# One memory for the rows of both graph-attention layers, and the first layer's softmax taken in groups

## The chip, the cores and the metric

The kernel runs on one core of a Trainium2 chip. The metric is the device time of one execution in microseconds (us). A core has five engines that run their own lists of instructions and meet at semaphores: TensorE (PE) multiplies matrices into PSUM, VectorE (DVE) and ScalarE (ACT) work elementwise on SBUF and PSUM, GpSimd (POOL) does small work and here mainly issues gathers, and SyncE (SP) issues plain DMA transfers. Everything is in 32-bit floats.

## The reference

The graph has 10,000 nodes with 768 features and 170,000 directed edges, sorted by destination and with self loops among them (the layer adds one more loop for each node). Two graph-attention layers follow each other, each with a layer norm and a residual product, and one last norm closes:

```python
def gat_conv(x, src, dst, W, a_src, a_dst, bias, heads):
    xl = (x @ W).reshape(n, heads, -1)
    e = leaky_relu((xl * a_src).sum(-1)[src] + (xl * a_dst).sum(-1)[dst], 0.2)
    e = exp(e - segment_max(e, dst)[dst])          # softmax over a node's edges
    alpha = e / (segment_sum(e, dst)[dst] + 1e-16)
    return segment_sum(xl[src] * alpha, dst) + bias

h1 = relu(layer_norm(gat_conv(x, W1, 4 heads x 256))) + (x @ Wr1 + br1)    # 1024 wide
h2 = layer_norm(gat_conv(h1, W2, 1 head x 768)) + (h1 @ Wr2 + br2)         # 768 wide
out = plain_norm(x + h2)
```

## The kernel before

The 10,000 nodes are put in order of their number of edges and cut into 79 tiles of 128 nodes. A tile has one node on each partition and as many **slots** as its busiest node has edges: slot k of a tile is a 128-row gather, row p being the features of the k-th neighbour of node p. There are 1377 slots in all, from 8 to 41 per tile.

**Three stages.** First x·W1 is computed for all nodes and stored as table 1 (a row has 1024 features, 4 + 4 attention terms and one more number, 1033 floats; 529 KB for 128 rows), while the order of the nodes is worked out beside it. Then layer 1 runs over the 79 tiles, gathers from table 1, and writes for each tile h1 and x (to `h1_d`, `x_d`) and a row of table 2 (770 floats; 394 KB for 128 rows). Then layer 2 runs over the tiles with gathers from table 2. The change touches layer 1 and the beginning of layer 2.

**Layer 1 for a tile of n slots.** In order of turn, n goes 8, 10, 11, ... up to 19 (turns 25 to 28), 20, 21 (32, 33), 22, 22, 23, 24, 26, 41 (turn 39), 27, 25, 24, 23, 22, 22, 21 (46) and down again to 9 (78). `Ring` holds the gathered rows in 29 slots that are reused round robin (`RING1`); `ring.fetch` on POOL (L425) issues the gather that refills a slot once the row in it has been weighed. The softmax weights of a tile come from `logits`: DVE adds the two terms of all n rows (L479), applies leaky relu (L189), takes the maximum (L483), subtracts it (L486), and ACT takes the exponential (L487); POOL copies the indices out and clears the row ends (L490, L491). `normalised` then divides by the sum (L504, L498 to L501). Since L479 reads all n rows, a tile's logits wait until its last row is in the ring.

The first four rows (`on_pe`) are summed on PE: ACT makes diagonal matrices of the weights (L730) and PE multiplies them with the rows into PSUM `acc` (L736). The others are summed by DVE in `weigh`: every fourth by four fused multiply-adds of 128x256 (L521), the other three of four by one 128x1024 addition (L517) after ACT has multiplied the row in place by its weights (L510). At the tile's end come the norm (L579, L581, L593, L595), relu and the residual (L807). PE also transposes h and x (L708), multiplies x by Wr1 (L172) and h by W2 (L829). The list of each engine is fixed in program order by the loop over k in `ordered_layer1`: three rows before the end of a tile (`LEAD`) stand the logits of the next tile, so that its first rows are ready when it begins.

**Tile 39** has 41 slots and the ring 29. It takes another way, `attend_parts`: the slots are cut into three groups, each with its own softmax whose sum is scaled to the new maximum (`fade`); nothing of the next tile is put into it, and the tiles 39 and 40 (27 slots, and 27 + `LEAD` is more than 29) do not get their logits ahead.

**From layer 1 to layer 2.** Layer 2's pool of buffers takes the memory of layer 1's, so its first instructions wait for the end of all of layer 1, the last of which is a store of table 2 (L768). Then SP loads h1 and x of the first two tiles of layer 2 (L911, L912), the tile's own row of table 2 (L454), and the broadcast vectors (L144); Wr2 is loaded earlier, into Wr1's place. DVE copies br1 out to a 128x1024 operand (L905), PE multiplies it by Wr2 (L172, 16 products), computes the residual of tile 0 (`residual`, L988 and L991: x + h1·Wr2), then, from the first rows, tile 0's sums (L946) and the residual of tile 1. Layer 2 has a ring of 41 slots (`RING2`), takes its tiles from few slots to many, and already has softmax groups, two for a tile of 26 slots or more (`cuts_of`, `PARTED2`). At the end of tile 0, DVE adds br1·Wr2 to a vector (L1066) from the PSUM buffer `q`.

Of the kernel before, what the change touches and what calls it, by code (L numbers as in the profile page):

```python
# [35 lines left out]
P = 128  # L36
BANK = 512
# [16 lines left out]
PARTED2 = 26  # L54

# [25 lines left out]
def gnn_kernel(ctx, tc, x, x_cols, src, dst, src_col, dst_col, W1, a_src1, a_dst1, b1, g1, be1, Wr1, br1,  # L81
# [359 lines left out]
    class Ring:  # L441
# [4 lines left out]
        def __init__(self, pool, table, row, size, own, at=None):  # L446
            self.table, self.size, self.own, self.issued = table, size, own, 0
            self.at = at or list(range(TOTAL))
            self.rows = pool.tile([P, size, row], F32, name="ring")
# [11 lines left out]

        def slot(self, q):
            return self.rows[:, q % self.size, :]

        def parts(self, lo, hi):

            while lo < hi:
                r = lo % self.size
                m = min(hi - lo, self.size - r)
                yield lo, lo + m, self.rows[:, r:r + m, :]  # L470
                lo += m
# [40 lines left out]
    def weigh(acc, row, e, dh, first=None, shared=False):  # L512


        if shared:
            c = e.shape[1] * dh
            nc.vector.tensor_add(acc[:, :c], acc[:, :c], row[:, :c])  # L517
            return
# [4 lines left out]

    def attend_parts(small, ring, acc, h_, ad, heads, dh, t, summed, between):


        c = heads * dh
        groups = -(-SLOTS[t] * 2 // ring.size)
        cuts = [FIRST[t] + SLOTS[t] * g // groups for g in range(groups + 1)]
        top = total = sums = None  # L530
        nc.vector.memset(acc[:, :c], 0.0)
        for lo, hi in zip(cuts, cuts[1:]):
            e, new = logits(small, ring, lo, hi, ad, heads, c, top)
            if lo == FIRST[t]:
                doubled(e, t)
            part = small.tile([P, heads], F32, name="part")
            nc.vector.reduce_sum(part, e.rearrange("p k h -> p h k"), axis=AX.X)
            if top is not None:
                nc.vector.tensor_add(acc[:, :c], acc[:, :c], sums[:, :c])
                fade = small.tile([P, heads], F32, name="fade")  # L540
                nc.vector.tensor_sub(fade, top, new)
                nc.scalar.activation(fade, fade, AF.Exp)
                for h in range(heads):
                    s = slice(h * dh, (h + 1) * dh)
                    nc.vector.tensor_scalar(acc[:, s], acc[:, s], fade[:, h:h + 1], None, op0=OP.mult)
                nc.vector.tensor_mul(fade, total, fade)
                nc.vector.tensor_add(part, part, fade)
            top, total = new, part
            m = min(ON_PE1, hi - lo - 1)
            pe = lo if hi == cuts[-1] else hi - m  # L550
            steps = summed(pe, e[:, pe - lo:], m)
            sums = next(steps)
            if pe == lo:
                for _ in steps:
                    pass
            alone = [q for q in range(lo, hi) if not pe <= q < pe + m]
            for k, q in enumerate(alone):
                shared = k >= len(alone) // 3
                if shared:
                    multiply(ring.slot(q), e[:, q - lo], dh)  # L560
                if k == len(alone) // 3 + 1:
                    for _ in steps:
                        pass
                weigh(acc, ring.slot(q), e[:, q - lo], dh, shared=shared)
                ring.fetch(q + 1 + ring.size)
            ring.fetch(hi + ring.size)
            between.pop(0)()
        nc.vector.tensor_add(acc[:, :c], acc[:, :c], sums[:, :c])
        divided(small, h_, acc, total, None, heads, dh)
# [111 lines left out]
    SLOTS1, FIRST1 = SLOTS, FIRST  # L681

# [3 lines left out]
    def ordered_layer1():  # L686
        nc.scalar.add_instruction(mybir.InstLoadActFuncSet(name=nc.get_next_instruction_name(), act_func_set_id=6, engine=nc.scalar.engine))
        with tc.tile_pool(name="b1", bufs=1) as pool, tc.tile_pool(name="small1", bufs=2) as small, \
# [3 lines left out]
            ring = Ring(pool, table1, R1, RING1, {})  # L692
# [25 lines left out]
            ring.fetch(RING1)  # L718
# [22 lines left out]
            def weights_of(t):  # L741

                n, m = SLOTS[t], on_pe(t)
                e, _ = logits(small, ring, FIRST[t], FIRST[t] + n, ring.slot(FIRST[t])[:, C1:C1 + H1], H1, C1)
                yield e
                normalised(small, e, H1, t)
                acc = ps_acc.tile([P, 2 * BANK], F32, name="acc")
                diagonals = pool.tile([P, ON_PE1 * H1, P], F32, name="diagonals")
                for lo, hi in ((0, min(m, 2)), (min(m, 2), m)):
                    summed(acc, diagonals, e, FIRST[t], lo, hi, m)  # L750
                    yield acc

# [18 lines left out]
            xT, moves = from_x(0)  # L771
            for move in moves:
                move()
            r = product(xT, wr1, C1, ps_r)
            for t in range(NT + 1):
# [3 lines left out]
                whole = live and n <= ring.size  # L779
                if whole and not ready:  # L780
                    ahead = weights_of(t)
                    ready += itertools.islice(ahead, 2)

                def multiplied(upto):
                    nonlocal done
                    while whole and done < min(upto, n):
                        if shared(t, done):
                            multiply(ring.slot(FIRST[t] + done), e[:, done], DH1)
                        done += 1

                if whole:
                    e, acc = ready
# [3 lines left out]
                for _ in ahead:  # L796
                    pass
# [544 lines left out]
```

## Time and profile before

| what | us |
|---|---|
| median of three runs | 5579.29 |
| the three runs | 5576.32, 5579.29, 5603.79 |
| the profiled execution: time | 5572.26 |
| the profiled execution: span in the trace | 5570.4 |
| first stage | 0 to 880 |
| layer 1 | 880 to 3412 |
| layer 2 | 3412 to 5570 |

| stage | PE busy | DVE busy | ACT busy | POOL busy | DMA share |
|---|---|---|---|---|---|
| first stage (880 us) | 844.63 | 481.76 | 353.62 | 422.02 | 0.38 |
| layer 1 (2532 us) | 2244.79 | 2196.78 | 1863.74 | 1544.97 | 0.91 |
| layer 2 (2158.4 us) | 1797.91 | 1591.10 | 597.77 | 1334.62 | 0.86 |

The profiled execution is 7.0 us below the median and 4.1 us below the fastest of the three runs. In the tables of the profile, "idle before" is the time in which an engine had nothing to run just before the group of instructions, and what stands behind the arrow is what ended it. Over all of layer 1, DVE waits 66.0 us in 12 waits for gathered rows at the logits (L479), and 46.5 us in 44 waits for PE's sum at the first row that it adds to it (L521).

### The profile page before, as it was taken

How to read it: one execution, taken by the hardware profiler on the slowest of the kernel's cores; microseconds unless marked ns; L12 is line 12 of the kernel's file. 1: busy time of each engine (PE TensorE's matmuls, PEld its weight loads, DVE VectorE, ACT ScalarE, POOL GpSimd, SP SyncE). 2: the span in 40 equal slices, each digit the busy share in tenths (PEclk: the TensorE clock that was granted, in tenths of full speed). 3: DMA queues.
4: the chain of work that ended last, by engine and by line, in shares of the span. 5: the costliest groups of instructions: out<-in, count | busy, mean ns of one | idle time of the engine just before them, and what ended most of it. 6: DMA issues, size and time to landing. Idle time of an engine off the chain costs nothing. (4 is left out here: it accounts for less than half of the span.)

```text
span 5570.4 us, 59760 instructions
## 1 busy us (share of the span) xinstructions
PE 4887.3 (88%) x15188; PEld 2896.9 (52%) x15191; DVE 4269.6 (77%) x7513; ACT 2815.1 (51%) x8193; POOL 3301.6 (59%) x3407
## 2 busy tenths in 40 slices
PE   9999996999999876689999999899988888887775
PEld 3444443555565544455555555565655555554544
DVE  5883344999999887789999995888876776766676
ACT  3443343777878776678877773333322222222222
POOL 2446455556666666566666653666665666666664
PEclk9999998999999987899999999999998888888887
DMA  4323536999999987899999986999888888888885
GB/s 156 123 94 89 91 97 234 323 345 354 364 366 371 350 325 255 314 342 369 370 367 361 339 310 230 334 336 329 323 322 287 307 298 301 295 291 294 293 293 183
DMA packets 474308, 1591.39 MB, mean 286 GB/s; under 512 B 118327, under 2 KB 122487, under 8 KB 473958
## 3 DMA queue, kind: packets, MB, share of 16 engines
q0 software_dynamic: 322384, 1286.62, 64.5%
q1 hardware_dynamic: 149520, 297.43, 15.8%
q10 hardware_dynamic: 2054, 3.42, 0.2%
q8 instruction: 128, 2.10, 0.1%
q14 instruction: 222, 1.82, 0.1%
HBM read 1431.80 MB, written 177.29 MB: 289 GB/s over the span
## 5 line engine op out<-in xcount | busy, mean ns | idle before, releaser
L425 POOL DMA_INDIRECT ring<-table,slots x2675 | 2664.3, 996 | 1631.5 <-issue 662.2
L521 DVE SCALAR_TENSOR_TENSOR acc<-ring,e,acc 128x512 f32<-128x512 f32 (+1 forms) x2530 | 1579.0, 624 | 149.4 <-PE acc L736 46.5
L510 ACT ACTIVATE ring<-ring,e 128x256 f32<-128x256 f32 x3284 | 1338.4, 508 | 2.3 <-issue 2.2
L517 DVE TENSOR_TENSOR acc<-acc,ring 128x1024 f32<-128x1024 f32 x801 | 986.5, 1232 | 70.5 <-DVE acc L517 1.4
L991 PE MATMUL big<-wr,w 128*128 128x512 f32 (+1 forms) x2464 | 872.0, 500 | 111.3 <-issue 109.8
L946 PE MATMUL big<-ring,diagonals 128*128 128x256 f32 x2754 | 758.5, 433 | 206.8 <-issue 168.0
L172 PE MATMUL big<-w,xT 128*128 128x512 f32 x1896 | 827.2, 598 | 23.3 <-DMA w<-in_W_dram 9.4
L172 PE MATMUL big<-wr,xT 128*128 128x512 f32 x1896 | 831.7, 595 | 0.2 <-issue 0.2
L829 PE MATMUL half<-w,hT 128*128 128x512 f32 (+1 forms) x2528 | 830.4, 486 | 0.0
L946 PEld LDWEIGHTS big<-ring,diagonals 128*128 128x128 f32 x2754 | 593.8, 219 | 371.5 <-issue 235.1
L991 PEld LDWEIGHTS big<-wr,w 128*128 128x128 f32 x2464 | 481.3, 196 | 471.4 <-issue 439.5
L945 ACT ACTIVATE diagonals<-ident,e 128x128 f32<-128x128 f32 x1377 | 423.5, 388 | 598.4 <-remote 180.3
L829 PEld LDWEIGHTS half<-w,hT 128*128 128x128 f32 x2528 | 477.8, 189 | 372.3 <-issue 334.4
L736 PE MATMUL acc<-ring,diagonals 128*128 128x256 f32 x1912 | 474.8, 406 | 201.9 <-ACT diagonals L730 198.0
L172 PEld LDWEIGHTS big<-w,xT 128*128 128x128 f32 x1896 | 362.7, 192 | 483.7 <-issue 464.9
L172 PEld LDWEIGHTS big<-wr,xT 128*128 128x128 f32 x1896 | 356.0, 191 | 419.4 <-issue 419.4
L736 PEld LDWEIGHTS acc<-ring,diagonals 128*128 128x128 f32 x1912 | 384.6, 204 | 285.0 <-ACT diagonals L730 219.0
L583 ACT ACTIVATE sd<-mv,eps 128x1 f32<-128x1 f32 x237 | 69.3, 293 | 696.9 <-DVE mv L581 444.4
L667 DVE TENSOR_TENSOR scr<-big,ad_b 128x1024 f32<-128x1024 f32 x79 | 96.7, 1224 | 378.4 <-ACT row L664 330.7
L730 ACT ACTIVATE diagonals<-ident,e 128x128 f32<-128x128 f32 x956 | 293.0, 388 | 173.3 <-DVE e L501 144.6
L672 POOL TENSOR_TENSOR row<-row,none 128x1024 f32<-128x1024 f32 x79 | 187.2, 2369 | 264.5 <-ACT row L664 261.5
L670 ACT ACTIVATE scr<-scr 128x256 f32<-128x256 f32 x632 | 253.5, 402 | 120.3 <-DVE scr L667 120.3
(185 smaller groups left out, 3445.0 us busy)
## 6 DMA issues: line engine op xcount, KB each, us to landing
ring<-table,slots POOLq DMA_INDIRECT x2675
table<-row SPq DMA_DIRECT2D x79, 516.0 KB
h_d<-hT SPq DMA_DIRECT2D x79, 512.0 KB
w<-h_d SPq DMA_DIRECT2D x77, 512.0 KB
table<-row SPq DMA_DIRECT2D x79, 385.0 KB
ring<-table SPq DMA_DIRECT2D x79, 385.0 KB
xT<-in_x_cols_dram SPq DMA_DIRECT2D x79, 384.0 KB
x_d<-xt SPq DMA_DIRECT2D x79, 384.0 KB
```

The costliest lines, as they stand in the source:

```text
L172: nc.tensor.matmul(p[:, c:e], aT[:, j, :], w[:, j, c:e], start=(j == 0), stop=(j == k - 1))
L425: nc.gpsimd.indirect_dma_start(out=to, out_offset=None, in_=table, in_offset=bass.IndirectOffsetOnAxis(ap=index, axis=0), **more)
L510: nc.scalar.activation(row[:, s], row[:, s], AF.Copy, scale=e[:, h:h + 1])
L517: nc.vector.tensor_add(acc[:, :c], acc[:, :c], row[:, :c])
L521: nc.vector.scalar_tensor_tensor(acc[:, s], row[:, s], e[:, h:h + 1], (acc if first is None else first)[:, s], op0=OP.mult, op1=OP.add)
L670: nc.scalar.activation(m[:, s], m[:, s], AF.Copy, accum_out=row[:, C1 + i * H1 + h:C1 + i * H1 + h + 1])
L730: nc.scalar.activation(diagonals[:, k * H1 + i, :], ident, AF.Copy, scale=e[:, k, i:i + 1])
L736: nc.tensor.matmul(acc[:, c:d], diagonals[:, k * H1 + i, :], ring.slot(q + k)[:, c:d], start=(k == 0 and c % BANK == 0), stop=(k == m - 1 ...
L829: nc.tensor.matmul(q, hT[:, j, :], w2[:, j, c:c + q.shape[1]], start=(j == 0), stop=(j == K1 - 1))
L945: nc.scalar.activation(diagonals[:, (k - lo) % G, :], ident, AF.Copy, scale=e[:, k - lo, :])
L946: nc.tensor.matmul(to, diagonals[:, (k - lo) % G, :], ring.slot(at + k)[:, ON_PE2:C2], start=False, stop=(k == n - 1), skip_group_check=True)
L991: nc.tensor.matmul(r[:, c:d], hT[:, j, :], wr2[:, j, c:d], start=False, stop=(j == K1 - 1 and d < C2), skip_group_check=True)
```

## The change

1. `mem`, one SBUF tile of 29 x 1033 floats outside of both layers' pools, holds both rings. Layer 2's ring has 38 of its 41 slots there and three in a tile of its own; `Ring` takes a list of views and finds a slot by `place`. Where a tile's rows go over the border between the views, its logits have one L479 more.
2. `begin_layer2` stands in layer 1's last turn (t = 79, which has only the rest of tile 78). SP's list gets there the loads of h1 and x for layer 2's first two tiles, into the end of `mem`, and the load of Wr2. DVE computes br1·Wr2 as a sum over eight blocks of Wr2, weighted by br1 per partition, and PE needs only two products with a matrix of ones to add it up over the partitions (16 before). The residuals of tiles 0 and 1 both stand ahead of tile 0's sums.
3. Layer 1's softmax is taken in groups for tiles of 22 slots or more (`PARTED`): turns 34 to 45. The cuts are [0, 11, n] for 22 and 23 slots, [0, 13, n] for 24 to 27, and [0, 13, 27, 41] for turn 39 (a cut that would fall on a row which DVE multiplies itself is moved by one). The logits of a later group stand eight rows before its cut, the scaling five before. At the cut four multiply-adds scale the sum and add the row in one. `attend_parts` is gone: tile 39 goes the way of the others, and every tile gets its logits ahead.
4. At the beginning of layer 1, POOL gathers the eight rows of tile 0 first, then x of tile 1, then the rest of the ring.

```diff
+PARTED = 22
 ...
+        def place(self, q):
+            r = q % self.size
+            for v in self.views:
+                if r < v.shape[1]:
+                    return v, r
+                r -= v.shape[1]
 ...
+        if fade is not None:
+            for h in range(e.shape[1]):
+                s = slice(h * dh, (h + 1) * dh)
+                nc.vector.scalar_tensor_tensor(acc[:, s], acc[:, s], fade[:, h:h + 1], row[:, s],
+                                               op0=OP.mult, op1=OP.add)
+            return
 ...
-    def attend_parts(small, ring, acc, h_, ad, heads, dh, t, summed, between):
 ...
+    def begin_layer2(mem):
+        rest = mem.shape[1]
 ...
+        firsts = [(at_end(C1), at_end(D0)) for _ in range(min(2, NT))]
+        for t, (hT, xt) in enumerate(firsts):
+            nc.sync.dma_start(hT, h1_d[turns[t]])
+            nc.sync.dma_start(xt, x_d[turns[t]])
+        wr2 = wr1.rearrange("p k n -> p (k n)")[:, :K1 * C2].rearrange("p (k n) -> p k n", n=C2)
+        load(wr2, Wr2)
+        br, ones = at_end(C2), at_end(P)
+        yield
+        nc.vector.memset(ones, 1.0)
+        nc.vector.tensor_scalar(br, wr2[:, 0, :], br1_c[:, 0:1], None, op0=OP.mult)
+        for k in range(1, K1):
+            nc.vector.scalar_tensor_tensor(br, wr2[:, k, :], br1_c[:, k:k + 1], br, op0=OP.mult, op1=OP.add)
+        yield wr2, firsts, br, ones, rest
 ...
             xt = fetch_x(0)
-            ring.fetch(RING1)
+            ring.fetch(SLOTS[0])
 ...
+                for lo, hi in zip(cuts[1:], cuts[2:]):
+                    e, new = logits(small, ring, at + lo, at + hi, ad, H1, C1, top)
+                    fade = small.tile([P, H1], F32, name="fade")
+                    nc.vector.tensor_sub(fade, top, new)
+                    nc.scalar.activation(fade, fade, AF.Exp)
+                    yield
+                    part = small.tile([P, H1], F32, name="part")
+                    nc.vector.reduce_sum(part, e.rearrange("p k h -> p h k"), axis=AX.X)
+                    nc.vector.tensor_mul(total, total, fade)
+                    nc.vector.tensor_add(total, total, part)
+                    top = new
+                    if hi == n:
+                        nc.vector.tensor_scalar(total, total, 1e-16, None, op0=OP.add)
+                        nc.vector.reciprocal(total, total)
+                        nc.vector.tensor_mul(fade, fade, total)
+                        nc.vector.tensor_mul(e, e, total[:, None, :].to_broadcast([P, hi - lo, H1]))
+                    yield lo, (e, fade)
+
+            def cuts_of(t):
+                n = SLOTS[t]
+                groups = 1 if n < PARTED else -(-2 * n // ring.size)
+                cuts = [n * g // groups for g in range(groups + 1)]
+                return [c + (0 < c < n and not shared(t, c)) for c in cuts]
 ...
             xT, moves = from_x(0)
+            xt = fetch_x(1)
+            ring.fetch(RING1)
 ...
-                if whole and t + 1 < NT and SLOTS[t + 1] + LEAD <= ring.size:
+                if live and t + 1 < NT:
                     ahead = weights_of(t + 1)
-                for k in range(n if whole else 0):
+                for k in range(n):
+                    if k + 2 * LEAD + 2 in cuts[1:-1]:
+                        next(later)
+                    if k + LEAD + 2 in cuts[1:-1]:
+                        lo, es_lo = next(later)
+                        es[lo] = es_lo
 ...
-            brT = at_end(C1).rearrange("p (k n) -> p k n", n=P)
-            nc.vector.tensor_copy(brT, br1_c[:, :, None].to_broadcast([P, K1, P]))
 ...
-            q = product(brT, wr2, C2)
-            rs = {0: residual(0)}
+            q = ps_big.tile([P, 2 * BANK], F32, name="big")
+            for c in range(0, C2, BANK):
+                d = min(C2, c + BANK)
+                nc.tensor.matmul(q[:, c:d], sums_of, br[:, c:d], start=True, stop=True)
+            rs = {t: residual(t) for t in range(2)}
 ...
                 if not t:
-                    rs[1] = residual(1)
                     ring.fetch(RING2)
 ...
+        with tc.tile_pool(name="rows", bufs=1) as rows_pool:
+            mem = rows_pool.tile([P, RING1 * R1], F32, name="ring")
+            ordered_layer2(mem, ordered_layer1(mem))
```

## The prediction

> **What bounds the kernel now.** I read the busy shares by slices first, then stretches of layer 1 by engine, then what DVE waits for in the worst of them, then DVE's timeline there and at the change of layers. No engine is full over the whole span, so each stage has to be read for itself.
>
> ```profile
> PE   9999996999999876689999999899988888887775
> DVE  5883344999999887789999995888876776766676
> PEclk9999998999999987899999999999998888888887
> DMA  4323536999999987899999986999888888888885
> ```
>
> The dip in slices 14 to 18 of all four rows is where layer 1 has its tiles of 22 to 41 slots. By stretches (columns: PE, PEld, DVE, ACT, POOL busy; PE's granted clock; DMA share; GB/s):
>
> ```profile
> 1901.50:2109.70 208.20, 152.48 (x494) 92.64 (x492) 172.97 (x244) 150.15 (x396) 125.12 (x136) 0.86 0.90 333
> 2109.70:2195.20 85.50, 50.21 (x169) 34.80 (x170) 60.15 (x118) 53.12 (x153) 55.35 (x55) 0.76 0.55 193
> 2195.20:2454.80 259.60, 195.45 (x628) 121.67 (x628) 213.63 (x309) 189.28 (x503) 155.90 (x171) 0.86 0.90 324
> 2524.30:2716.40 192.10, 180.41 (x619) 108.93 (x619) 174.57 (x257) 158.30 (x428) 131.13 (x140) 1.00 0.99 370
> ```
>
> The first three are turns 34 to 38, turn 39 (41 slots) and turns 40 to 45; the fourth is six ordinary tiles of 19 and 20 slots. There DVE is idle 17.5 us, 2.9 a tile. In the heavy twelve it is idle 553.3 - 446.8 = 106.5 us, 8.9 a tile, while PE and DMA have room too: everybody waits for somebody. DVE's waits in 1901.5 to 2454.8:
>
> ```profile
> DVE e L479 <- DMA ring<-table,slots: 37.7, 9, 7.7
> DVE acc L521 <- PE acc L736: 19.6, 11, 4.3
> DVE h L517 <- ACT ring L510: 6.9, 15, 1.7
> DVE e L479 <- issue: 3.0, 2, 2.5
> ```
>
> With 2.6 us of POOL's, the logits (L479) cost 43.3 us. Why they wait is seen in DVE's timeline, with POOL's last gathers before it:
>
> ```profile
> 2003.38 3.91 DVE L517 TENSOR_TENSOR acc<-acc,ring 128x1024 f32<-128x1024 f32 x3
> 2012.55 0.26 DVE L479 TENSOR_TENSOR e<-ring 128x96 f32<-128x96 f32 x1 [5.26 <-DMA ring<-table,slots]
> ...
> 2004.88 0.99 POOL L425 DMA_INDIRECT ring<-table,slots  x1 [0.34 <-DVE acc L517]
> ```
>
> The next tile's 24 rows and the current tile's last three fill the ring of 29 but for two: the last rows could be asked for only when DVE had just freed their slots, and DVE then stands 5.26 us with three rows of work behind the L479. The second place is the change of layers:
>
> ```profile
> 3391.10 1.22 DVE L807 SCALAR_TENSOR_TENSOR h<-h,big 128x1024 f32<-128x1024 f32 x1
> 3412.66 0.70 DVE L905 COPY ring<-br_c 128x1024 f32<-128x1024 f32 x1 [20.34 <-DMA table<-row]
> 3435.43 0.17 DVE L479 TENSOR_TENSOR e<-ring,ad 128x8 f32<-128x8 f32 x1 [7.26 <-DMA ring<-table,slots]
> 3449.45 0.17 DVE L479 TENSOR_TENSOR e<-ring,ad 128x10 f32<-128x10 f32 x1 [3.01 <-DMA ring<-table,slots]
> 3456.58 0.95 DVE L1066 TENSOR_TENSOR be<-be,big 128x768 f32<-128x768 f32 x1
> ```
> ```profile
> 3384.00:3412.00 28.00, 24.97 (x79) 13.88 (x77) 7.76 (x8) 4.28 (x10) 0.00 (x0) 1.00 0.42 160
> 3412.00:3460.00 48.00, 44.99 (x144) 27.46 (x144) 15.05 (x39) 6.39 (x22) 28.53 (x30) 0.96 0.98 351
> ```
>
> DMA is 0.42 full in the 28 us before 3412 and 0.98 in the 48 us after: what is moved across 3412 shortens the full part.
>
> **Groups, what they add.** A cut costs DVE one more set of logits. A whole set for 88 to 96 numbers takes 2.4 us by the pitches at 2012.55 to 2016.66 (nine instructions, less the rows between them). Halves take 1.6 us (first) and 2.85 us (second, with its fade arithmetic), from the rows of 160 to 250 ns for 4 to 56 numbers: +2.07. The cut row is four multiply-adds at a 0.525 us pitch (2.1 us) in place of an addition of 1.3: +0.8. So 2.9 us a cut; eleven tiles: +32. Turn 39 has 10 rows of 2.1, 25 additions of 1.3, two fades of 2.1, 7.3 of logits and 6.2 of tail, 71 us and some 70 of it busy, against 60.15: +10. DVE's busy time becomes 446.8 + 42 = 489.
>
> **What they return.** The first group has 11 to 13 rows, all gathered 14 or more rows earlier. The second's rows are needed eight rows before the cut of the tile itself: later than now by three rows, the tail and one or two rows, some 4.6 + 6.2 + 4.5 + 2 = 17 us, against waits of 7.7 us at most; turn 39's third group has nine rows, some 14 us. The 43.3 us go, but for 1.6 at the uncut turn 46, and so do turn 39's own waits. DMA doesn't stop it: the twelve tiles move 333 x 208.2 + 193 x 85.5 + 324 x 259.6 = 170 MB, 459 us at 370 GB/s. What is late next is PE's sum at L521: 19.6 us, some 12 above the 0.6 a tile of ordinary tiles, because PE's clock is 0.86. PE stays idle over 10 us a tile, so I keep the 12. Twelve tiles at 2.9 us of idle time make 35: 489 + 35 = 524, with the 12 us 536. Turn 33, whose end holds turn 34's logits, gives 2.8 more. So -32 to -20; I take **-20**, since the row with PE's wait is of these very tiles. If half of the logits' waits come back (21), it is 0; that is the upper bound, -32 the lower.
>
> POOL's 22 more instructions (index copies of 0.39 and clears of 0.21 us) lie in a POOL that is 60% busy there; they stand before gathers that have 14 rows to spare. ACT's 0.2 us exponentials of the fades have three rows (4 us) before use. If that cover fails, 0.6 us a cut, 8 us in all.
>
> VectorE: DVE Perf Modes of the Trainium skill, section on the TRN2 errata, speaks against cutting: each instruction pays a fixed time, measured there as about 150 cycles at 0.96 GHz, and operands of 512 elements and more are advised. An estimate by it for some 164 more DVE instructions in layer 1 (of 196 in the whole list) is 26 us, where the rows above give 42; the groups would then bring -36 and the whole -40.
>
> **The change of layers.** Two h and two x (1.8 MB) and a row (0.39 MB) leave the full stretch. At 351 GB/s that is 6.2 us, so tile 0's rows land at about 3428.5, tile 1's at 3442.5. PE's product with br1 falls from 12.3 us to 1.3; residuals 0 and 1 (24.5 us together) can run from 3409.4, when PE is free, to about 3435, beside the gathers. The residual of tile 2 waits for the PSUM buffer that L1066 (end 3457.5) frees, now at about 3451. SP's four loads (0.32 to 0.51 us each) stand before Wr2's load, which lands at about 3399 now, and wait for ring slots of turn 77, free by then. DVE's eight products of 128x768 at 1.02 us (the duration of such an operation at L595) are 8.2 us behind Wr2, inside DVE's 20.34 idle, ending at 3407; nothing else of DVE's is due. If the loads delay Wr2 by their own 4.9 us, PE begins 3 us later. The residual of tile 1 now stands before tile 0's sums on PE, which then start at 3435, as now. I take **-6.5**, in -10 to -3.
>
> **The beginning of layer 1.** DVE stands at the first row of tile 0, though its rows and weights are there:
>
> ```profile
> 927.91 2.06 DVE L521 SCALAR_TENSOR_TENSOR acc<-ring,e,acc 128x256 f32<-128x256 f32 x4 [18.72 <-remote]
> ```
>
> It ends when the 29 gathers of the first ring have been worked off. Now 30 gathers stand there, with x (384 KB, 1 us of DMA at 351 to 410 GB/s and 1.25 us of POOL's pitch). I take **+1**; the wait can be lengthened by 4 or, if its cause goes, shorten by 18. Early x of tile 1 gains nothing: its transposes start without a wait now.
>
> **Layer 2's border** between its views falls into some 24 tiles, one more L479 of about 0.2 us, on a DVE with 26% idle: **+1**, from 0 to 5.
>
> The sum: -20 - 6.5 + 1 + 1 = -24.5 us on the profiled execution's 5572.3 gives 5547.8. That execution is 7.0 us below the median, so against medians I expect **5555**.
>
> **Rivals.** (B, slower) The second group's gathers are late as well. For this, 17 us of slack must be used up: the gathers in question landed 4 to 7.5 us after issue, but DMA at 0.99 in the ordinary stretch shows that queues can stand full. Place: the second L479 of each cut tile. It decides when less than 37 of DVE's 106.5 idle us come back (42 - 4.5). If the 43.3 us stay and only turn 39's 10 us go: +32 - 4.5 = +27.5, 5607; with a wait twice in some tiles, 5620.
> (C, full return) PE gets its clock back and its waits at L521 fall to ordinary ones, while the change of layers gives 10: -32 - 10 and a start that loses some of its 18.7 us: -47, 5532. Against it: PE's idle time in these tiles remains.
> (D, transfers hidden anyway) Gathers of layer 2 still wait for table 2's last store, and if they rather than bytes set 3435 and 3449, the change of layers gives 0: -18, 5561; with Wr2 late, 5564.
>
> **How the numbers follow.** The forecast has 0.55; the distances of its terms from their bounds, added as squares, are 23 us down and 21 up, and eight tenths of that make its own range 5537 to 5573; B 0.16, C 0.17, D 0.12. Half a per cent, about what a measurement can tell here, is 27.9 us. Beyond it lie C and a bit under half of the forecast's range (0.25): faster 0.42. Slower: three quarters of B, 0.12. The same: 0.46. The range leaves out the far third of C (0.05) and most of B (0.12): 5526 to 5595.
>
> **What the changed profile would show.** Right: waits of L479 for gathers in turns 34 to 45 below 8 us; those twelve tiles in 524 to 540 us; turn 39 at some 71 us; L521's waits for PE still near 20; the first L479 of layer 2 about 36 us after the end of turn 78's L807 (43 now) and the second 50 (57 now); DVE idle 12 us, not 20, behind that L807. Wrong: a wait of several us at the second L479 of the cut tiles (B), a clock of 0.95 there (C), or 18.72 us that has changed by much.

## The result and the profile after

| | before | after |
|---|---|---|
| median of five runs | 5576.32 us | 5554.23 us |
| the five runs | 5572.16 to 5603.79 | 5544.56 to 5556.51 |
| profiled execution: time and span | 5572.26, 5570.4 | 5554.23, 5551.8 |

The ratio is 0.995 (95% interval 0.9927 to 0.9972): 22 us faster. The forecast was 24.5 us, but the stages of the two traces show that several of its terms were wrong in opposite directions. A turn of layer 1 is counted up to the start of its last DVE operation (L807 before, L847 after), a tile of layer 2 up to the start of its residual's addition.

| stretch | before | after | difference | forecast |
|---|---|---|---|---|
| to the last product of the first stage | 876.5 | 879.9 | +3.4 | 0 |
| from there to turn 21 of layer 1 | 636.3 | 636.0 | -0.3 | +1 |
| turns 22 to 32 | 351.9 | 351.7 | -0.2 | 0 |
| turns 33 to 45 | 590.1 | 556.5 | -33.6 | -20 |
| turns 46 to 78 | 936.3 | 935.1 | -1.2 | 0 |
| from turn 78 to tile 4 of layer 2 | 145.9 | 143.5 | -2.4 | -6.5 |
| the rest of layer 2 | 2033.4 | 2049.1 | +15.7 | +1 |

The groups gave two thirds more than forecast, and layer 2, where from tile 4 on only the ring's border is new, gave part of it back. The page's rows by slices:

```profile
PE   9999996999999885789999997999888888877765
DVE  5883244899998999899999995988777776666776
PEclk9999998999999997899999998999998888888887
DMA  4333636899999998999999977999888888888885
```

DVE had 8, 8, 7, 7, 8 in slices 14 to 18 and has 9, 9, 9, 8, 9; DMA's 9, 8, 7, 8, 9 became 9, 9, 8, 9, 9. PE's dip stays, and with it that of its clock, with its lowest point at turn 39. The same stretches as before (turns 34 to 38, 39, 40 to 45, and six ordinary tiles; columns as before):

```profile
1901.60:2103.80 202.20, 157.32 (x507) 96.34 (x506) 184.00 (x324) 154.52 (x421) 129.47 (x150) 0.88 0.96 343
2103.80:2174.80 71.00, 32.62 (x108) 20.11 (x108) 64.07 (x109) 51.77 (x139) 44.27 (x51) 0.74 0.71 233
2174.80:2424.00 249.20, 191.35 (x616) 118.06 (x615) 225.48 (x396) 188.93 (x512) 157.56 (x184) 0.87 0.95 337
2493.30:2684.10 190.80, 179.11 (x614) 107.78 (x613) 174.57 (x257) 158.10 (x428) 130.04 (x139) 1.00 1.00 372
```

DVE's busy time in the twelve tiles is 184.00 + 64.07 + 225.48 = 473.6 us (446.8 before, so +26.8, where +42 was forecast), its idle time 522.4 - 473.6 = 48.8 (106.5 before). Of this idle time the waits that the profile lists make 10.1 us (76.7 before); the other 38.7 us (29.8 before) are gaps between instructions, too short for that list, and there are 160 instructions more. What DVE waits for in 1901.6 to 2424.0:

```profile
DVE acc L537 <- PE acc L731: 8.0, 7, 1.6
...
DVE e L489 <- issue: 0.4, 2, 0.2
DVE e L489 <- DMA ring<-table,slots: 0.2, 1, 0.2
```

The logits (L489) wait 0.6 us instead of 43.3, and the wait for PE's sum has fallen with them, from 19.6 to 8.0. DVE's timeline at the change of layers:

```profile
3359.09 1.22 DVE L847 SCALAR_TENSOR_TENSOR h<-h,big 128x1024 f32<-128x1024 f32 x1
...
3366.00 7.35 DVE L675 SCALAR_TENSOR_TENSOR ring<-wr,br_c,ring 128x768 f32<-128x768 f32 x7
...
3400.93 0.17 DVE L489 TENSOR_TENSOR e<-ring,ad 128x8 f32<-128x8 f32 x1 [13.55 <-DMA ring<-table,slots]
...
3414.97 0.17 DVE L489 TENSOR_TENSOR e<-ring,ad 128x10 f32<-128x10 f32 x1 [10.23 <-DMA ring<-table,slots]
```

br1's products are hidden as forecast: they end at 3373.4, and PE takes them up at 3377.5, after its last product with W2. But the first logits come 41.8 us after L847's start and the second 55.9, against 44.3 and 58.3 before: 2.5 us earlier, not 6.9. SP's list shows transfers that moved up with them:

```profile
3380.27 0.32 SPq L145 DMA_DIRECT2D out<-shift  x1
...
3387.70 3.35 SPq L455 DMA_DIRECT2D ring<-table  x4
3391.09 0.50 SPq L936 DMA_DIRECT2D w<-h_d  x1
3391.64 0.51 SPq L937 DMA_DIRECT2D w<-x_d  x1
```

Here the own rows of four more tiles and h1 and x of tile 2 are issued 28.6 to 32.6 us after L847's start, ahead of tile 0's logits. In the kernel before they followed 37.3 to 46.8 us after L807's start (3428.43 to 3437.92), the four rows still ahead of its tile 0's logits, x of tile 2 behind them. The stretch from 1 us ahead of the first gather to tile 0's logits, before and after (columns as above):

```profile
3412.00:3435.43 23.43, 22.02 (x61) 12.08 (x62) 1.79 (x4) 0.00 (x0) 13.43 (x15) 0.93 0.94 296
3380.00:3400.93 20.93, 20.93 (x65) 12.10 (x64) 1.10 (x3) 0.00 (x0) 13.31 (x14) 1.00 0.87 282
```

That is 6.9 MB before and 5.9 MB after: 1.0 MB less, where 2.2 MB had been taken out. DMA was not full in it after the change, so bytes alone don't set these logits.

At the beginning of layer 1 DVE now waits 4.33 us at tile 0's first row, where it stood 18.72:

```profile
919.82 2.06 DVE L537 SCALAR_TENSOR_TENSOR acc<-ring,e,acc 128x256 f32<-128x256 f32 x4 [4.33 <-issue]
...
934.35 0.23 DVE L514 TENSOR_SCALAR e<-e,loops 128x4 f32<-128x4 f32 x1 [4.81 <-issue]
```

but tile 0's logits come 6.1 us later (913.00 against 906.89), 3.4 us of it because the first stage ended later; the first gather was issued at 894.24 instead of 887.25. At tile 1, L514 waits 4.81 us with nothing recorded that it waits for; the kernel before has no such wait there. The sum over that stretch is nil.

### The profile page after: what moved, and what is told of

It is laid out like the page before. It is cut to its first block, busy times and chain, and to the rows that moved or that the text cites. A ratio compares the mean times of both kernels' runs of the same rounds, so it can differ in the third digit from the quotient of the medians.

```text
span 5551.8 us, 59930 instructions
## 1 busy us (share of the span) xinstructions
PE 4861.0 (88%) x15096; PEld 2874.0 (52%) x15099; DVE 4307.7 (78%) x7709; ACT 2815.7 (51%) x8211; POOL 3288.0 (59%) x3429
## 5 line engine op out<-in xcount | busy, mean ns | idle before, releaser
L537 DVE SCALAR_TENSOR_TENSOR acc<-ring,e,acc 128x256 f32<-128x256 f32 (+1 forms) x2570 | 1598.5, 622 | 129.7 <-PE acc L731 35.1
L533 DVE TENSOR_TENSOR acc<-acc,ring 128x1024 f32<-128x1024 f32 x815 | 1003.7, 1232 | 70.3 <-issue 2.1
L1016 PE MATMUL big<-wr,w 128*128 128x512 f32 (+1 forms) x2464 | 887.9, 506 | 140.8 <-issue 139.4
L971 PE MATMUL big<-ring,diagonals 128*128 128x256 f32 x2754 | 743.3, 428 | 188.4 <-issue 142.9
L173 PE MATMUL big<-w,xT 128*128 128x512 f32 x1896 | 828.1, 599 | 25.7 <-DMA w<-in_W_dram 9.9
L731 PE MATMUL acc<-ring,diagonals 128*128 128x256 f32 x1848 | 457.7, 404 | 198.7 <-ACT diagonals L725 166.1
L731 PEld LDWEIGHTS acc<-ring,diagonals 128*128 128x128 f32 x1848 | 367.9, 202 | 281.2 <-ACT diagonals L725 188.1
```

Of the source, the lines that this page charges most:

```text
L173: nc.tensor.matmul(p[:, c:e], aT[:, j, :], w[:, j, c:e], start=(j == 0), stop=(j == k - 1))
L537: nc.vector.scalar_tensor_tensor(acc[:, s], row[:, s], e[:, h:h + 1], (acc if first is None else first)[:, s], op0=OP.mult, op1=OP.add)
L731: nc.tensor.matmul(acc[:, c:d], diagonals[:, k * H1 + i, :], ring.slot(q + k)[:, c:d], start=(k == 0 and c % BANK == 0), stop=(k == m - 1 ...
L971: nc.tensor.matmul(to, diagonals[:, (k - lo) % G, :], ring.slot(at + k)[:, ON_PE2:C2], start=False, stop=(k == n - 1), skip_group_check=True)
L1016: nc.tensor.matmul(r[:, c:d], hT[:, j, :], wr2[:, j, c:d], start=False, stop=(j == K1 - 1 and d < C2), skip_group_check=True)
```

## The experiments

The later runs went to four other chips. From turn 22 on, layer 1 takes the same time on all of them within some 4 us in each stretch. Layer 2 doesn't: from tile 4 to the end the kernel before took 2033.4 us in the first chip's trace and 1716.3 on the third. Nor does the beginning of layer 1: with the changed beginning, the stretch up to turn 21 took 636.0 to 636.5 us on the first and fourth chip, whose layer 2 is the long one, and 624 to 626 on the other three. So medians are only compared within a chip, and stretches across chips only from turn 22 to turn 78.

### The changed kernel again, on a second chip

> The changed kernel once more, unaltered, to see which of its stages repeat. In the first trace layer 1 ended 32.0 us earlier than before, but the whole span only 18.6 us: the tiles of layer 2 from about 4500 to 4940 us lost 12 us, and the first stage, whose code is the same, took 3.4 us more. Theory A: these are variations of unchanged code; layer 1's tiles 34 to 45 take 522 us again (within 2), layer 1 from its first tile's end to its last gives 32 us less than before within 3, and the 12 us of layer 2 differ from run to run by several us. Theory B: the loss in layer 2 is of the change (its ring's border, other slots): it returns within 3 us at the same tiles.

Measured: 5198.44 us against 5235.81 of the kernel before, ratio 0.9928 (0.9915 to 0.9942): 37 us. Turns 34 to 45 took 523.4 us (522.4 in the first trace). Layer 2 from tile 4 took 1717.9 us, and there was no loss at the tiles in question. Theory A on this chip, except that the chip itself differs by far more than the "several us"; whether the loss returns on the first chip was not tried.

### The groups alone

The changed kernel with its parts 1, 2 and 4 undone, so that only this is left of the diff:

```diff
+PARTED = 22
-                if whole and t + 1 < NT and SLOTS[t + 1] + LEAD <= ring.size:
+                if live and t + 1 < NT:
                     ahead = weights_of(t + 1)
 ... (weights_of in groups, fade in weigh, no attend_parts)
```

> Only the softmax groups of layer 1 are put into the kernel before; the memory of the rows, the change of layers and the beginning of layer 1 are as before. Theory A: all but a few us of the gain is the groups': turns 34 to 45 take 522 us, and the median lies 3 us above to 3 us below the changed kernel's, some 5552 to 5558. Theory B: layer 2's 12 us are lost by the new ring or the early loads, so this kernel keeps the groups' 32 us whole and comes out near 5545. Rival C: the change of layers is worth the forecast 6.5 us: 5561.

Measured on the second chip: 5210.52 us, ratio to before 0.9953 (0.9939 to 0.9967), 25 us faster; the changed kernel beside it 37 us. So here a third of the gain is not the groups'. By stages: turns 34 to 45 523.6 us, as in the changed kernel; from the first stage to turn 21 631.2 us against 625.4; from turn 78 to tile 4 of layer 2 138.4 against 131.4. B fails: layer 2 from tile 4 took 1714 us here and 1717.9 in the changed kernel. A fails too, since the beginning of layer 1 and the change of layers are worth 6 and 7 us on this chip; C named the second of these, which is half of the 12 us.

### The kernel before again, and the changed one beside it, on a third chip

> The kernel before, unaltered, for a second trace of it by stages. Theory A: turns 34 to 45 take 553 us (within 2), so that the groups are worth 31 us and turn 33 two more on every chip; from the end of the first stage to the end of turn 21 it takes 636 us like in its first trace, or 631 like the kernel with the groups alone, whose beginning is the same: the difference between these two would be chance. Rival: the heavy tiles' waits depend on the chip's DMA, and the 553 differ by 10 us or more.

> The changed kernel unaltered, as the reference for the three runs beside it. On the chip of the first four runs the kernel before took 5236 us and the changed one 5198, 37 us less, while on the first chip it was 22 us less; layer 1's stages were the same on both chips within 2 us. Theory A: turns 34 to 45 take 522 to 524 us here as well; what is left of the difference between chips lies in the beginning of layer 1 and in layer 2.

Measured: 5238.40 (5240.97 over the 15 runs of the kernel before that went beside these) and 5199.56 us; the changed kernel's ratio is 0.9924 (0.991 to 0.9938). By stages, before and changed: to the end of the first stage 878.4 and 878.9; to turn 21 631.9 and 625.1; turns 33 to 45 586.9 and 556.8; turn 78 to tile 4 137.8 and 132.4; the rest of layer 2 1716.3 and 1716.6. So turns 33 to 45 give 30.1 us here and 33.6 on the first chip. Turns 34 to 45 alone took 550.2 us, 3 us less than in the first trace and just outside theory A's 2; the changed kernel's 522.7 is as expected. The beginning took 631.9 us, like the kernel with the groups alone, and not 636.3 as in the first trace. What the early x of tile 1 is worth, PE's timeline of the kernel before shows on this chip:

```profile
926.73 3.78 PE L736 MATMUL acc<-ring,diagonals 128*128 128x256 f32 x8 [10.56 <-ACT diagonals L730]
941.83 1.51 PE L708 MATMUL half<-ident,xt 128*128 128x128 f32 x6 [11.31 <-DMA xt<-in_x_dram,order]
943.59 1.97 PE L708 MATMUL half<-ident,h 128*128 128x128 f32 x8 [0.25 <-ACT xT L709]
```

PE waits 11.31 us for x of tile 1, whose gather stood behind the ring's, and ACT's row multiplications stand behind the copy of its transposes (DVE waited 8.02 us for them at 945.44). With x gathered early the transposes run at 933.24 without a wait, and tile 2 ends 6.3 us earlier. In the first trace the same wait didn't show, because DVE had stood 18.72 us at tile 0 and everything behind it was late anyway; on the third chip that wait was 4.12 us. It ended at 916.22 there, while the ring's gathers were issued until 926.48, so there it isn't their end that DVE waits for, as the prediction read it from the first trace. On the first and fourth chip the changed beginning gains nothing against the first trace's 636.3: in three traces L514 of tile 1 waits 4.7 to 5.0 us with nothing recorded, where it starts without a wait on the third, and the time is lost by tile 2. The kernel before was traced only once on a chip of that kind, so whether the 18.72 us return there stays open.

### h1 and x of layer 2's first tiles loaded late

```diff
-        for t, (hT, xt) in enumerate(firsts):
-            nc.sync.dma_start(hT, h1_d[turns[t]])
-            nc.sync.dma_start(xt, x_d[turns[t]])
```

(and loaded in layer 2's `fetch_x` again).

> As the changed kernel, but h1 and x of layer 2's first two tiles are loaded in layer 2 again (1.8 MB). Theory A: the stretch behind table 2's last store is bound by bytes, so layer 2's first logits come 1.8 MB / 350 GB/s = 5 us later, tile 4's end too, and the median is 3 to 6 us above the changed kernel's beside it. Rival: the transfers are hidden behind the gathers' own latency: within 1 us.

Measured on the third chip: 5199.19 us, the changed kernel's 5199.56. Layer 2's first logits came 43.6 us after L847's start instead of 41.9, tile 4 133.8 instead of 132.4 us after it: 1.4 to 1.7 us, a third of what the bytes make, and nothing at the end. The rival is nearer. (Kernels with the changed layer 2 reached tile 4 between 131.4 and 132.9 us on the second, third and fifth chip, so of the 1.4 us at tile 4 not much stands clear of that.)

### br1·Wr2 on PE again

```diff
+        brT = at_end(C1).rearrange("p (k n) -> p k n", n=P)
 ...
+        nc.vector.tensor_copy(brT, br1_c[:, :, None].to_broadcast([P, K1, P]))
 ...
+            q = product(brT, wr2, C2)
```

> As the changed kernel, but PE multiplies the spread br1 by Wr2 again (16 products, 12.3 us), and DVE's eight products of 128x768 are gone. Theory A: PE's 11 us before the residuals of tiles 0 and 1 lie in the time in which the first gathers land, but these two residuals (24 us) already fill that time, so tile 0's sums on PE come up to 11 us later and tile 0's end with them; of this some 3 to 8 us are left at tile 4, and the median is 2 to 6 us above the changed kernel's. Rival: layer 2 is bound by gathers from its first tile on; then PE's 11 us cost nothing, within 1 us.

Measured on the third chip: 5201.73 us (5199.15 to 5206.75), 2 us above the changed kernel, with overlapping runs. PE's tile 0 sums began at 3403.43, 52.7 us after L847's start, instead of 44.5; tile 4 ended 1.6 us later, 1.1 us beyond the latest of the traces with the changed layer 2. The mechanism is A's, but less is left at tile 4 than it named, and the median alone would not show it.

### The broadcast vectors early too

Layer 2's five vectors loaded behind Wr2 in layer 1's last turn:

```diff
+        vectors = [at_end(C2) for _ in range(5)]
+        for b, v in zip(vectors, (shift, b2, g2, be2, br2)):
+            nc.sync.dma_start(b, bass.AP(tensor=v.tensor, offset=v.offset, ap=[[0, P], [1, C2]]))
 ... (layer 2 adds or copies them into their places)
```

> As the changed kernel, but the five broadcast vectors of layer 2 (5 x 384 KB, 1.97 MB) are loaded behind Wr2 in layer 1's last turn, into the end of the rows' memory, and only added or copied into their places in layer 2. Theory A, as for the early h1 and x: the bytes leave a full stretch, layer 2's first logits come some 4 to 5 us earlier and tile 4 ends 2 to 5 us earlier, but what is left at the end is within 3 us of the changed kernel's, as it was when h1 and x were put back. Rival: the whole 5.6 us stay to the end.

Measured on a fourth chip, which is of the first one's kind in layer 2: 5532.36 us against 5564.26 (ratio 0.9942, 0.9923 to 0.9961). The first logits came 40.5 and the second 49.5 us after L847's start. In the run with six rows on PE (below), which has the changed kernel's layer 2 on the same chip, it was 41.6 and 55.8, so 1.1 and 6.3 us are gained. But tile 4 came at 143.1 us, there at 140.8 (143.5 in the first trace). The gain reaches the second tile's rows and is lost again within three tiles; the rival is wrong. Theory A's 4 to 5 us at the first logits and its gain at tile 4 didn't come either: 1.97 MB fewer gave 1.1 us, as 1.8 MB more had cost 1.7. The changed kernel itself was not run on this chip, so its median can't be set beside this one.

### Cuts in turns 39 and 40 alone

```diff
-PARTED = 22
+PARTED = 27
```

> Only turns 39 and 40 (41 and 27 slots) are cut; the other ten tiles of 22 to 26 slots have one softmax again. From the two traces' tile periods: turns 39 and 40 gave 20 us, the ten others, with turn 33, about 14. Theory A: the waits of the logits for gathers come back in turns 34 to 38 and 41 to 45 (some 25 us of them), less 10 cuts of 2.1 us of DVE's work: 10 to 14 us above the changed kernel, 5564 to 5568. Rival: tile 39's own way through the parts was all of it, then it equals the changed kernel within 4 us; or the cuts of the others cost more than their waits, then it is faster.

Measured on the second chip: 5215.81 us, 17 above the changed kernel. Turns 33 to 45 took 575.2 us against 558.2. Turn 39 alone kept its 70 us. DVE's waits in turns 34 to 45:

```profile
DVE e L489 <- DMA ring<-table,slots: 24.4, 9, 5.2
DVE acc L537 <- PE acc L731: 17.7, 12, 2.5
DVE e L489 <- POOL ring L501: 4.3, 2, 2.2
```

The logits' waits are back with 28.7 us, and with them PE's, 17.7 instead of the 9.2 of the changed kernel on this chip. PE's clock is 0.87, 0.73 and 0.86 in the three stretches here, 0.88, 0.73 and 0.87 there. So the clock doesn't explain that difference. My reading is that a good part of it is the same wait seen one step on: late logits, late diagonals, late sum. That part isn't measured by itself, since a cut alone also takes some of PE's wait away where no logits are late (0.6 us a tile in turns 46 to 57, two runs below), which over ten tiles would be up to 6 of the 8.5 us between the two runs. The cut of the ten tiles from 22 to 26 slots is worth 17 us, somewhat more than expected, because this was left out.

### The price of a cut where there is no wait

```diff
-PARTED = 22
+PARTED = 18
```

> Measures the price of a cut where there is no wait to be had back: the 24 tiles of 18 to 21 slots (turns 22 to 33 and 46 to 57) are cut as well. By DVE's busy time in the changed kernel's turns 34 to 45 a cut costs 2.1 us, 2.4 with the gaps between its instructions: 24 times that is 50 to 58 us, less some 5 us of waits at turns 32 and 33: 5600 to 5608. By the forecast's 2.9 us a cut it is 70 - 5 = 65: 5619. If DVE's additional work is hidden in these tiles, whose DMA share is 0.99, it is near 5554.

Measured on the second chip: 5289.90 us, 91 above the changed kernel: 3.8 us a cut, more than either number. In turns 46 to 57 DVE has no late logits, but:

```profile
DVE part L765 <- ACT e L497: 25.7, 12, 4.3
```

In these twelve tiles it waits at the scaling of the second group for ACT's exponential. ACT's timeline there shows why:

```profile
2565.60 1.71 ACT L520 ACTIVATE ring<-ring,e 128x256 f32<-128x256 f32 x4
2567.52 0.86 ACT L704 COPY xT<-half 128x512 f32<-128x512 f32 x2 [0.21 <-PE half L703]
2568.27 1.71 ACT L520 ACTIVATE ring<-ring,e 128x256 f32<-128x256 f32 x4
2569.87 0.23 ACT L497 ACTIVATE e<-e 128x40 f32<-128x40 f32 x1
```

DVE's part of the logits was ready at 2567.2, and the exponential stands in ACT's list behind a copy of x and row multiplications. With 18 to 21 slots the logits of the second group stand at row 1 or 2, when ACT has all of the tile's beginning before it; with 22 and more they stand at row 3 or later.

### The same with the scaling two rows later

```diff
-                    if k + LEAD + 2 in cuts[1:-1]:
+                    if k + LEAD in cuts[1:-1]:
```

> As the run with tiles of 18 slots and more cut, but a later group's scaling stands three rows before its cut instead of five, so DVE has two more rows to add before it reads the exponentials. In that run the 24 more cuts cost 92 us, 3.8 each; in twelve of them DVE waited 25.7 us at the scaling (L765) for ACT's exponential (L497), which stands in ACT's list behind copies and row multiplications. Theory A: that wait is the difference to the 2 us of DVE's work: turns 22 to 32 fall from 396 to 372 us (352 without cuts) and turns 46 to 57 from 429 to 406 (382 without), and L765 waits less than 5 us in turns 46 to 57. Rival: the tiles are short of something else (DMA at 0.93, PE's clock at 0.93): DVE's wait moves to another place and these stretches stay within 8 us.

Measured on a fifth chip: 5233.43 us, ratio to before 0.9991 (0.9982 to 1.0001). Turns 22 to 32 took 366.9 us, turns 46 to 57 401.4, below A's numbers; L765 has no wait left:

```profile
L765 DVE TENSOR_REDUCE part<-e 128x4 f32<-128x40 f32 (+2 forms) x12 | 2.6, 215 | 0.0
```

So two rows' distance is worth 57.5 us over these turns and turn 33 (862.3 before it, 804.8 with it), 2.4 a cut. A cut's own price is (804.8 - 767.6)/24 = 1.6 us, with 767.6 us for these turns in the changed kernel. That is less than the 2.1 us of DVE's work because the waits for PE at L537 go as well: 0.2 us in turns 46 to 57, where the changed kernel has 7.0.

### Six rows on PE in the cut tiles

```diff
-                return min(max(SLOTS[t] // 2 - 5, 1), ON_PE1, SLOTS[t])
+                return min(max(SLOTS[t] // 2 - 5, 1), ON_PE1 if SLOTS[t] < PARTED else 6, SLOTS[t])
 ...
-                        nc.scalar.activation(diagonals[:, k * H1 + i, :], ident, AF.Copy,
+                        nc.scalar.activation(diagonals[:, k % ON_PE1 * H1 + i, :], ident, AF.Copy,
 ...
-                for lo, hi in ((0, min(m, 2)), (min(m, 2), m)):
+                for lo, hi in ((0, max(min(m, 2), m - 2)), (max(min(m, 2), m - 2), m)):
```

> As the changed kernel, but in the twelve cut tiles PE sums six rows instead of four (the diagonal matrices of the last two in the buffers of the first two). It asks what bounds these tiles now that the waits are gone. Theory A: DVE, with DMA close behind (share 0.96, 0.71, 0.95 in turns 34 to 38, 39, 40 to 45, and full at 1.00 in the tiles after them). DVE loses 2 rows a tile, some 3 us, PE gains 2 x 1.9 us with 10 us of idle time: turns 34 to 45 fall from 523 us by 10 to 25, where DMA stops them; 10 to 25 us below the changed kernel's 5199 if the chip is the same. Rival: DVE's first addition waits for PE's six rows: 2 us more at each L537 for PE, and nothing is gained or some 10 us lost.

Measured on the fourth chip: 5544.86 us. Turns 34 to 45 took 538.6 us, 16 more, though DVE worked only 440.6 us:

```profile
DVE part L765 <- ACT e L497: 34.2, 8, 7.0
DVE acc L537 <- PE acc L731: 20.2, 6, 4.1
DVE part L765 <- issue: 6.6, 1, 6.6
```

The rival's direction, with ACT's list as the larger part: rows 0 to 5 are PE's, so between the logits (at row 3 with 22 slots) and the scaling (at row 6) DVE has none or few of its own to add.

### Six rows on PE with the later scaling

```diff
-                cuts = [n * g // groups for g in range(groups + 1)]
+                cuts = [n * g // groups + 2 * (g == 1 and groups == 2) for g in range(groups + 1)]
 ...
-                    if k + LEAD + 2 in cuts[1:-1]:
+                    if k + LEAD in cuts[1:-1]:
```

> As the run with six rows on PE in the cut tiles, with the same later scaling, and the cut of tiles with two groups two rows later. There turns 34 to 45 took 538.6 us against 523 with four rows on PE: DVE worked 33 us less, but waited 41 us at the scaling for ACT and 20 at L537 for PE. Theory A: ACT's place in the chain is the cause, and with four rows to add in between it is gone: DVE's 441 us, some 35 us of gaps and some 20 us for PE make 496; DMA's 170 MB at 372 GB/s make 457: 495 to 508 us, and the kernel lies 15 to 28 us below the changed one. Rival: PE's six rows are the cause, they hold ACT's copies of the transposes and DVE's first addition alike: 525 us or more.

Measured on the fifth chip: 5197.08 us (5187.77 to 5200.95), ratio to before 0.9919 (0.9905 to 0.9933); the changed kernel had 0.9928 and 0.9924 on two other chips. Turns 34 to 45 took 519.7 us. ACT's wait is gone, but:

```profile
DVE acc L537 <- PE acc L731: 43.0, 12, 5.8
```

PE's sum of six rows is what DVE waits for now. The rival's cause with a better time than it named. No version that was tried is clearly faster than the changed kernel.

## Why the prediction was right, and where it was wrong

**The total** was right on the first chip: -24.5 forecast, -22 in the medians, -18.6 in the profiled executions. It was right by terms that cancel, which is luck: the groups gave 13.6 us more than taken, the change of layers 4.1 less, layer 2's rest took 14.7 more, and the first stage 3.4. On the second and third chip the same change is worth 37 and some 40 us.

**What a cut adds** was too high. Forecast: 2.9 us a cut and 10 for turn 39, 42 in all; measured in DVE's busy time 2.1 a cut, 3.9 for turn 39, 26.8 in all. The pitches that I added up hold the small gaps between instructions, so they aren't busy time: the gaps beside it grew by 8.9 us, and busy time and gaps together by 35.7, 6 less than forecast. Also, turn 39's old way had work of its own to lose (its memset, two scalings of the sum, three additions of PE's part). The estimate from the Trainium skill's page VectorE: DVE Perf Modes, section on the TRN2 errata (a fixed time for each instruction), was 26 us, and the measured 26.8 us of busy time agree with it. The 8.9 us of gaps are not in that estimate.

**What the groups return** was right in its first step: the logits' waits went from 43.3 to 0.6 us, and 17 us of slack were enough. Wrong was the step "What is late next is PE's sum at L521 ... so I keep the 12". The clock stayed at 0.88, as I said, but the wait fell to 8.0 us, and with the cuts of ten tiles undone it was 17.7 again at almost the same clock. It followed the cuts and the logits' waits, not the clock. The lower bound of 524 us for the twelve tiles was the right end; measured 522.4, and 522.7 to 523.8 in the other traces with the same groups. But it was met by errors that cancel: it stood for 489 us busy and 35 idle, and 473.6 and 48.8 were measured. Turn 39's 71 us came out as 71.0, and as 70 in the other traces.

**Rival B** did not come true at its place: the second L489 waits 0.2 us. A wait in place of the one removed exists all the same, at the scaling (L765), for ACT's exponential; it shows only where the logits stand at row 1 or 2 or where DVE has no row in between (25.7 and 34.2 us in the two runs). I had covered it with "three rows (4 us) before use", which holds for the cut tiles of the changed kernel, where L765 has no wait.

**Rival C** gave its time for turns 33 to 45 (-32 named, -33.6 measured), but not by its first cause: the clock did not come back. Its second did come true without it: the waits for PE's sum fell to 8.0 us in twelve tiles, 0.7 a tile, where ordinary tiles have 0.6. **Rival D** holds for h1 and x on the third chip, where putting them back left the median as it was.

**The change of layers**: the products on DVE were hidden, and the residuals ran while the first rows came, as forecast. The step that failed is "At 351 GB/s that is 6.2 us" (the landing times given with it, 3428.5 and 3442.5, are even 6.9 us earlier): the first rows came 2.5 us earlier. Later transfers of SP's list moved up into the room, but DMA wasn't full there either (0.87 at 282 GB/s), and 1.8 MB put back and 1.97 MB taken out moved the first logits by 1.7 and 1.1 us only. So bytes don't set these rows alone; what else does stays open. On the third chip tile 4 came 5.4 us earlier than before; putting h1 and x back cost 1.4 us of that there, and br1 back to PE 1.6. The other 2.4 us were not taken apart.

**The beginning of layer 1**: "Early x of tile 1 gains nothing" was wrong in general. It was read from a trace in which an 18.72 us wait, which the third chip doesn't have, had hidden PE's wait for that x. On the second and third chip the beginning gives 6 to 7 us. On the first it gives nothing (-0.3), though the 18.72 us had fallen to 4.33: another wait, 4.81 us at L514 with nothing recorded, stands behind it.

**Layer 2's border** was worth what I took or less: 1716.3 before, 1716.6 and 1717.9 after on the second and third chip.

**Not settled**: the +15.7 us in layer 2's rest on the first chip. The list of instructions there is the same but for the border. On the fourth chip, whose layer 2 is of the same kind, the same stretch took 2022.7 and 2013.0 us in two kernels with the changed layer 2, and the 17 executions of the kernel before there run from 5546.56 to 5580.06, so executions of this kind spread by more than the change's 22 us; but before and after were traced once each on the first chip, and I can't show that this one difference is spread. The first stage's 3.4 us are in unchanged code, and 875.4 to 880.5 us were seen over all runs.

## What to carry to other kernels

When one engine's wait for data goes, look at the next engine's wait in the same chain before keeping it in the sum: a late input can show up again as a late result of another engine. An instruction that is split and moved must be followed into every in-order list on its way (here ACT's), and its distance in time to the reader counted in work that the reader really has in between. A single wait of many us at a stage's beginning should not be trusted from one trace on one chip, neither as a cost nor as a cover.

## What the runs showed that was not expected

Layer 2 has two speeds, by chip, and so has the beginning of layer 1; the rest of layer 1 has one. The kernel before, PE's waits in 3540 to 5540 us on the first chip:

```profile
PE big L946 <- issue: 155.1, 106, 4.7
PE big L991 <- issue: 109.8, 103, 3.1
```

and in 3525 to 5210 us on the third chip, the same tiles:

```profile
PE big L946 <- ACT diagonals L945: 109.3, 31, 14.1
PE big L950 <- ACT big L976: 31.2, 3, 16.2
```

On the first, PE stops some 200 times, for 1.1 to 1.5 us on average, with nothing recorded that it waits for, and DMA has a share of 0.86 at 302 GB/s. On the third there is no such stop, and DMA has 0.97 at 359 GB/s. From tile 4 on this is 2033.4 against 1716.3 us. What stops PE there stays open. For a change like this one it matters in that its parts outside of the groups, 12 us of 37 on the second chip, could not be seen on the first.
